# Two changes to the loads of a selective-scan kernel: the order of four partition quarters, and the layout of B and C in DRAM

## The chip, the cores and the metric

The kernel runs on one core of one Trainium2 chip. The metric is the device time of one execution in microseconds (us); the median of three runs of the kernel before is 12483.95 us (12473.74 to 12504.42). A core has TensorE (PE, matrix products), VectorE (DVE), ScalarE (ACT), GpSimd (POOL) and SyncE (SP), which here only issues DMA transfers. ACT issues transfers too. Sixteen DMA engines move the data between DRAM and the on-chip memory of 128 partitions (SBUF).

## The reference, cut to what matters

Two image layers are followed by two token layers. An image layer is a selective scan over 4 images of 64 x 64 pixels in four directions (K = 4), with E = 192 channels and 16 states:

```
delta = softplus(dt_projs(dts) + bias)            # (image, direction, channel, step)
h     = exp(delta * A) * h + delta * u * B        # 16 states, one step after another
y     = sum over states of h * C  (+ u * D)
```

`u` is the convolved and activated input, read in each direction's order; B and C depend on image, direction and step. The four directions are added, normalised, gated and projected. The token layers are linear attention and a feed-forward network in quantised numbers; they aren't touched by the change.

## The kernel before, in words

Images are taken in pairs. One pair in one image layer is a *phase*; there are four, one after the other (2 pairs, 2 layers). Each has three parts: `prepare` (normalisation, convolution, projection; all results go to DRAM), `scan_phase` (the recurrence) and `finish` (summing, norm, gate, output projection), where the finish of one phase runs between the steps of the next one's `prepare`. The token layers come last.

**How the scan is tiled.** G = 8 groups (4 directions x 2 images) times 16 states make the 128 partitions. Partition 32a + 4g + s holds group g and state 4a + s, so a *quarter* of 32 partitions has all groups and four states. A *unit* is 12 channels (EB) times 512 steps (TC); a *chunk* is 16 units, all 192 channels of 512 steps; 8 chunks make the 4096 steps, 128 units a phase.

**What a unit does.** `load` fills a tile `h` of 128 x 12 x 512 numbers (3 MB in all) with delta * u: the same values for all 16 states, so every quarter takes the same 8 rows of DRAM, each repeated for four partitions. POOL multiplies h by B (`times_b`, L406, four instructions of three channels). PE spreads delta to all partitions (`replicate`, L412), ACT takes exp(A * delta) in place (`decay`, L416), DVE runs the recurrence along 512 steps (`scan`, L423, one instruction per channel). PE contracts h with C (`contract`, L441), ACT evicts (`evict`, L453), SP stores y in four transfers (`store`, L461).

**du in DRAM.** `steps` writes delta * u twice, as copies 0 and 1, one on ACT's queue and one on SP's (L319). `load_quarters` (L396) reads quarter 0 from copy 0, quarter 3 from copy 1, and quarters 1 and 2 in one transfer from both copies, quarter 1 from copy 0 and quarter 2 from copy 1. Each is split into two halves of six channels: two transfers of 768 KB and four of 384 KB per unit. The order is in L387.

**B and C in DRAM.** `steps` writes 32 rows of 512 numbers, B's 16 states and C's 16, to `ph.bc[chunk][group]` by ACT's queue (L301), one transfer for each group. In the scan, `load_b` and `load_c` fetch a chunk's B or C as four transfers of 64 KB on SP, one per quarter (L344).

**What sets the order.** In `scan_phase` the program order is kept on each engine, so SP's order is as written: at the last channel (n = 11) of unit `at`, four stores of y of unit at−1; in some units a load of b (unit 8 of a chunk, for the next chunk) or of c (the last unit, for the chunk after the next); then the load of unit at+3, that is `dlt` (delta, one transfer of 288 KB, L376) and six transfers of h. The tile h has four buffers, so the load of unit at+3 takes the buffer that unit at−1 has just left. In `prepare` and `finish` a scheduler orders the instructions by its own estimates. POOL starts on a unit half a unit ahead of DVE in program order (B_LEAD = 6).

At the start of a phase SP issues: b of chunk 0, the load of unit 0, c of chunk 0, the loads of units 1 and 2, c of chunk 1 (L489 to L494).

Of the kernel before, what the change touches and what calls it, by code (L numbers as in the profile page):

```python
# [9 lines left out]
F32 = mybir.dt.float32  # L10
# [14 lines left out]
NS = 16  # L25
R = 6
K = 4
G = 2 * K
PAD = HW + 2
TC = 512  # L30
NC = L // TC
# [42 lines left out]
def rows(t):  # L74

    if len(t.shape) == 2:
        return t.rearrange("p (r w) -> p r w", w=HW)
    return t.rearrange("p h (r w) -> p h r w", w=HW)
# [49 lines left out]
class Scans:  # L128
# [19 lines left out]
    def prepare(self, ph):  # L148

        nc, cst, a, pre = self.nc, self.cst, self.a, ph.pre  # L150
        ph.gs = self.keep.tile([C, 2, 2], F32, name="gs", bufs=3)
        ph.delta = [
            self.dram.tile([NP16, G, E, TC], BF16, name="delta", bufs=2 * NC) for _ in range(NC)
        ]


        ph.du = [
            self.dram.tile([2, G, E + PITCH, TC], F32, name="du", bufs=2 * NC) for _ in range(NC)
        ]
        ph.bc = [self.dram.tile([G, 2 * NS, TC], F32, name="bc", bufs=2 * NC) for _ in range(NC)]  # L160
        ph.ud = self.dram.tile([C, 2, HW, 2, 64], F32, name="ud")
        ph.y = self.dram.tile([64, G, 2, 2, NEB, 16 * EB], F32, name="y")
        x = ph.x_in[ph.pair]

        with self.tc.tile_pool(name="prep", bufs=1) as wp, self.tc.tile_pool(
            name="steps", bufs=2
        ) as sp:

            def load(name, shape, at=0):
                t = wp.tile([at + shape[0]] + shape[1:], F32, name=name)  # L170
                nc.sync.dma_start(t[at:], a[pre + name])
                return t

            xp = load("x_proj", [C, 2, 2, XD2])
            dt_w = load("dt_w", [XD2 - 2 * NS, 2, E], at=2 * NS)
            conv_b = load("conv_b", [C, 2])
            ds = load("Ds", [C, 2, K])
            dsum = wp.tile([C, 2], F32, name="dsum")
            nc.vector.tensor_reduce(dsum, ds, mybir.AxisListType.X, ALU.add)
            yield  # L180


            st = wp.tile([C, 2, 8, 6], F32, name="st")
            with self.tc.tile_pool(name="stats", bufs=2) as rp:
                for hl in range(8):
                    raw = rp.tile([C, 8, 2, 64], F32, name="raw")
                    nc.sync.dma_start(raw, x[:, hl * 8 : hl * 8 + 8])
                    for i in range(2):
                        nc.vector.bn_stats(st[:, i, hl], raw[:, :, i])
                    yield  # L190
            for i in range(2):
                mv = wp.tile([C, 2], F32, name="mv")
                nc.vector.bn_aggr(mv, st[:, i].rearrange("p c s -> p (c s)"))
                ps = self.bank()
                nc.tensor.matmul(ps[:C, :1], cst.group, mv[:, 0:1], start=True, stop=True)
                gs = ph.gs[:, i]
                nc.vector.tensor_copy(gs[:, 0:1], ps[:C, :1])
                d = wp.tile([C, 1], F32, name="d")
                nc.vector.tensor_tensor(d, mv[:, 0:1], gs[:, 0:1], ALU.subtract)
                nc.vector.scalar_tensor_tensor(d, d, d, mv[:, 1:2], ALU.mult, ALU.add)  # L200
                ps = self.bank()
                nc.tensor.matmul(ps[:C, :1], cst.group, d, start=True, stop=True)
                ln = wp.tile([C, 2], F32, name="ln")
                neg_rsqrt(nc, cst, ps[:C, :1], ln[:, 0:1], gs[:, 1:2], ln[:, 1:2])
                nc.vector.tensor_scalar_mul(gs[:, 1:2], gs[:, 1:2], -1.0)
                yield
            in_w = wp.tile([C, E], F32, name="in_w")
            nc.sync.dma_start(in_w, a[pre + "in_proj_w"][:, :E])
            taps = wp.tile([C, 9, E], F32, name="taps")
            nc.sync.dma_start(taps, a[pre + "conv_w"].unsqueeze(0).broadcast_to([C, 9, E]))  # L210

            nc.vector.tensor_tensor(
                taps, taps, in_w.unsqueeze(1).broadcast_to([C, 9, E]), ALU.mult
            )

            xc = [wp.tile([C, 2, L], F32, name="xc", bufs=2) for _ in range(2)]
            yield from self.convolve(ph, 0, x, xc[0], taps, conv_b, dsum)
            ph.beside = 0.5
            other = self.convolve(ph, 1, x, xc[1], taps, conv_b, dsum)
            for i in range(2):  # L220
                for c in range(NC):
                    for k in range(2):
                        yield from self.steps(ph, sp, xc[i], xp, dt_w, i, k, c)
                        for _ in range(2):
                            next(other, None)
                            yield
                for _ in other:
                    yield
                ph.beside = 1.7
# [52 lines left out]
    def steps(self, ph, sp, xc, xp, dt_w, i, k, c):  # L282


        nc, cst = self.nc, self.cst
        u = scan_view(xc, k, c)
        ps = self.bank()
        for h in range(2):
            nc.tensor.matmul(rows(ps[:XD2]), xp[:, k, h], u[:, h], start=h == 0, stop=h == 1)  # L289
        xd = sp.tile([XD2, TC], F32, name="xd")  # L290

        nc.scalar.activation(xd[:XD], ps[:XD], AF.Identity, bias=cst.one_row[:XD])  # L292
        nc.scalar.activation(
            xd[64:], view(ps[64:XD2], TC - 1, (-1, TC)), AF.Identity, bias=cst.one_row[64:]
        )
        yield
        both = []
        for back in range(2):
            at = 64 * back
            g, cc = 2 * (k + 2 * back) + i, NC - 1 - c if back else c  # L300
            nc.scalar.dma_start(ph.bc[cc][g], xd[at : at + 2 * NS])  # L301
            both.append((g, cc, scan_view(xc, k + 2 * back, cc), self.p_d.tile([C, 2, TC], F32, name="d")))
        for m in range(2):
            for back, (_, _, _, ps) in enumerate(both):
                part = slice(64 * back + 2 * NS, 64 * back + XD)
                nc.tensor.matmul(  # L306
                    ps[:, m], dt_w[part, k, m * C : (m + 1) * C], xd[part], start=True, stop=True
                )
        yield
        for g, cc, u, ps in both:  # L310
            delta = sp.tile([C, 2, TC], F32, name="dl")
            parts = sp.tile([C, NP16, 2, TC], BF16, name="parts")
            du = sp.tile([C, 2, TC], F32, name="du_sb")
            nc.scalar.activation(delta, ps, AF.Softplus)  # L314
            nc.scalar.copy(parts[:, 0], delta)
            nc.vector.tensor_tensor(rows(du), rows(delta), u, ALU.mult)  # L316
            nc.vector.tensor_tensor(delta, delta, parts[:, 0], ALU.subtract)  # L317
            for copy, queue in enumerate((nc.scalar, nc.sync)):
                queue.dma_start(ph.du[cc][copy, g, :E].rearrange("(h e) t -> e h t", h=2), du)  # L319
            nc.gpsimd.tensor_copy(parts[:, 1], delta)  # L320
            nc.vector.tensor_tensor(parts[:, 2], delta, parts[:, 1], ALU.subtract)  # L321
            for h in range(2):
                nc.scalar.dma_start(
                    ph.delta[cc][:, g, h * C : (h + 1) * C].rearrange("n q t -> q n t"),
                    parts[:, :, h],
                )
            yield
# [10 lines left out]
        ph.carry = self.keep.tile([128, E], F32, name="carry")  # L338
        ph.b, ph.c, ph.cw = {}, {}, {}

    def load_states(self, t, of):

        for a in range(4):
            self.nc.sync.dma_start(t[32 * a : 32 * a + 32], of[:, 4 * a : 4 * a + 4])  # L344

    def load_b(self, ph, c):
        ph.b[c] = self.units.tile([128, TC], F32, name="b")
        self.load_states(ph.b[c], ph.bc[c][:, :NS])

    def load_c(self, ph, c):  # L350
        ph.c[c] = self.units.tile([128, TC], F32, name="c")
        self.load_states(ph.c[c], ph.bc[c][:, NS:])

    def weights(self, ph, c, op):

# [25 lines left out]
    def load(self, u):  # L381

        nc, ph = self.nc, u.ph
        u.h = self.units.tile([128, EB, TC], F32, name="h", bufs=4)
        self.load_delta(u)
        n = EB // 2
        for first, quarters in ((1, 2), (0, 1), (3, 1)):  # L387
            for e in range(0, EB, n):
                self.load_quarters(u, e, n, first, quarters)

# [593 lines left out]
```

## Time and profile before

| What | us |
|---|---|
| median of 3 runs | 12483.95 |
| profiled execution, its own time | 12443.48 |
| its span, first to last instruction | 12441.7 |
| PE busy | 10107.0 |
| DVE busy | 9376.9 |
| POOL busy | 7386.0 |
| ACT busy | 7185.6 |
| the four scan phases together | 7660 |
| the parts before, between and after them | 4755 (the last, 1206, holds the token layers) |

The page gives one profiled execution. A group of instructions is named by its line, its engine and the tiles it writes and reads (`h<-du` is a transfer from du to h); behind the bar stand its busy time, the mean ns of one, and the idle time of its engine just before it with what ended most of it. The chain is found by going back from the last instruction to whatever released it, again and again; "SPq" is time in which SP issues or waits.

### The profile page before, as it was taken

The page shows a single profiled execution, that of the slowest core. Times are in us where ns is not written, and L with a number is a line of the kernel's source. Part 1 is how long each engine was busy: PE and PEld are TensorE (multiplying, and loading weights), DVE is VectorE, ACT ScalarE, POOL GpSimd, SP SyncE. Part 2 cuts the span into 40 slices and gives each one's busy share as a digit, 9 for nine tenths or more (in the row PEclk, how much of TensorE's full clock was granted, in tenths as well). Part 3 has the DMA queues.
Part 4 walks back from the last instruction along what each step waited for, and adds up shares of the span by engine and source line. Part 5 has one row for each costly group of instructions (what it writes and reads, how often), then busy time and mean ns, then how long its engine had stood idle before and what let it go on. Part 6 is the DMA issues. An engine that isn't in the chain of part 4 may idle for free.

```text
span 12441.7 us, 340858 instructions
## 1 busy us (share of the span) xinstructions
PE 10107.0 (81%) x147008; PEld 4972.1 (40%) x147008; DVE 9376.9 (75%) x9235; ACT 7185.6 (58%) x11815; POOL 7386.0 (59%) x2316
## 2 busy tenths in 40 slices
PE   7758888879878888879878888888878888887777
PEld 2224444433334444433334444443334444444333
DVE  2479999963569999982469999992459999993567
ACT  2456666644456666653456666663446666662556
POOL 0159999950149998960139899880129989990000
PEclk8665565669675555659775656558776655557787
DMA  3567676754667676764566777664567666663110
GB/s 92 172 227 247 244 248 247 248 168 140 213 205 246 245 247 244 250 200 128 176 215 244 246 247 249 243 226 125 174 202 249 244 243 245 245 244 122 30 21 11
DMA packets 882704, 2491.45 MB, mean 200 GB/s; under 512 B 279058, under 2 KB 561840, under 8 KB 737456
## 3 DMA queue, kind: packets, MB, share of 16 engines
q1 hardware_dynamic: 552496, 2163.38, 50.6%
q10 hardware_dynamic: 328704, 306.26, 8.5%
q8 instruction: 1158, 18.97, 0.7%
q14 instruction: 346, 2.83, 0.1%
HBM read 1955.42 MB, written 513.80 MB: 198 GB/s over the span
## 4 chain that ended last, share of the span: by engine, by line
DMA 53%; PE 20%; SPq 8%; DVE 7%; ACT 4%; issue 4%; POOL 3%; ACTq 1%; POOLq 0%; DVEq 0%
DMA h<-du 47%; PE c L260 8%; SPq L396 7%; POOL h L406 3%; PE f L591 2%; DVE h L423 2%; PE d L306 2%; DMA yk<-y 1%; PE c L289 1%; PE f L600 1%; POOL parts L320 1%; PE f L682 1%; DMA du<-du_sb 1%; PE y L441 1%; DVE parts L321 1%
## 5 line engine op out<-in xcount | busy, mean ns | idle before, releaser
L406 POOL TENSOR_TENSOR h<-h,b 128x1536 f32<-128x1536 f32 x2048 | 7016.6, 3456 | 780.6 <-DMA h<-du 369.0
L423 DVE TENSOR_TENSOR_SCAN h<-a,carry,h 128x512 f32<-128x512 f32 x5376 | 6356.7, 1259 | 391.8 <-POOL h L406 360.9
L416 ACT ACTIVATE a<-a,a_col 128x512 f32<-128x512 f32 x6144 | 4030.3, 662 | 1966.6 <-PE a L412 1814.4
L441 PEld LDWEIGHTS y<-h,cw 128*32 128x32 f32 x131072 | 2886.3, 145 | 3597.6 <-issue 1606.1
L441 PE MATMUL y<-h,cw 128*32 128x48 f32 x131072 | 3702.1, 269 | 438.0 <-ACT a L416 216.9
L412 PE MATMUL a<-dlt,rep 24*128 24x512 bf16 x6144 | 3319.4, 551 | 884.8 <-DVE h L423 782.1
L320 POOL CAST parts<-dl 96x1024 bf16<-96x1024 f32 x256 | 341.3, 1348 | 3092.1 <-DVE dl L317 2785.6
L316 DVE TENSOR_TENSOR du_sb<-dl,xc 96x1024 f32<-96x1024 f32 x256 | 397.3, 1577 | 1296.2 <-ACT dl L314 1234.8
L453 ACT COPY d<-y 128x384 f32<-128x384 f32 x2048 | 979.6, 478 | 485.7 <-PE y L441 432.7
L260 PE MATMUL c<-xn,taps 96*96 96x512 f32 x2304 | 1034.1, 609 | 73.5 <-DVE xn L245 71.0
L423 DVE TENSOR_TENSOR_SCAN h<-a,h 128x512 f32<-128x512 f32 x768 | 869.6, 1201 | 189.0 <-ACT a L416 110.6
L412 PEld LDWEIGHTS <-rep 24*128 24x128 bf16 x6144 | 471.9, 101 | 903.6 <-issue 451.0
L306 PE MATMUL d<-xd,dt_w 7*96 7x512 f32 x1024 | 520.8, 859 | 254.9 <-ACT xd L292 225.6
L260 PEld LDWEIGHTS c<-xn,taps 96*96 96x96 f32 x2304 | 382.6, 167 | 707.5 <-issue 628.7
L823 POOL MEMSET tn<- 1x4096 f32 x8 | 27.8, 3506 | 865.0 <-PE pa L843 514.7
L267 ACT ACTIVATE xc<-c,conv_b 96x512 f32<-96x512 f32 x128 | 87.3, 682 | 718.1 <-PE c L260 633.2
L591 PE MATMUL f<-yk,perm 128*128 128x384 f32 x1024 | 415.9, 546 | 99.6 <-DMA yk<-y 88.8
L314 ACT ACTIVATE dl<-d 96x1024 f32<-96x1024 f32 x256 | 252.0, 1017 | 400.9 <-DMA delta<-parts 234.5
L321 DVE TENSOR_TENSOR parts<-dl,parts 96x1024 bf16<-96x1024 f32 x256 | 366.9, 1455 | 153.2 <-POOL parts L320 153.1
L289 PE MATMUL c<-xc,x_proj 96*103 96x512 f32 x512 | 420.2, 958 | 4.2 <-ACT xc L267 4.2
L306 PEld LDWEIGHTS d<-xd,dt_w 7*96 7x96 f32 x1024 | 151.7, 212 | 542.4 <-ACT xd L292 295.8
L360 ACT ACTIVATE cw<-c,gmask 128x256 f32<-128x256 f32 x512 | 287.9, 573 | 126.2 <-DMA h<-du 65.9
(114 smaller groups left out, 5650.6 us busy)
## 6 DMA issues: line engine op xcount, KB each, us to landing
h<-du SPq DMA_DIRECT2D x1024, 768.0 KB
h<-du SPq DMA_DIRECT2D x2048, 384.0 KB
delta<-parts ACTq DMA_DIRECT2D x512, 288.0 KB
dlt<-delta SPq DMA_DIRECT2D x512, 288.0 KB
du<-du_sb SPq DMA_DIRECT2D x256, 384.0 KB
du<-du_sb ACTq DMA_DIRECT2D x256, 384.0 KB
y<-d SPq DMA_DIRECT2D x2048, 48.0 KB
yk<-y SPq DMA_DIRECT2D x256, 384.0 KB
```

The lines of the kernel that those rows point to most:

```text
L260: nc.tensor.matmul(rows(ps[:C]), taps[:, tap, h * C : (h + 1) * C], xn[:, ROWS * c + dy : ROWS * (c + 1) + dy, dx : dx + HW], start=tap == ...
L289: nc.tensor.matmul(rows(ps[:XD2]), xp[:, k, h], u[:, h], start=h == 0, stop=h == 1)
L306: nc.tensor.matmul(ps[:, m], dt_w[part, k, m * C : (m + 1) * C], xd[part], start=True, stop=True)
L321: nc.vector.tensor_tensor(parts[:, 2], delta, parts[:, 1], ALU.subtract)
L396: self.nc.sync.dma_start(u.h[32 * first : 32 * (first + quarters), e : e + n].rearrange("p e t -> p (e t)"), source.rearrange("a g e t -> ...
L406: self.nc.gpsimd.tensor_tensor(h, h, b, ALU.mult)
L412: self.nc.tensor.matmul(u.a[n], rep, u.dl[:, n], start=True, stop=True)
L416: self.nc.scalar.activation(u.a[n], u.a[n], AF.Exp, scale=u.ph.a_col[:, at : at + 1])
L423: self.nc.vector.tensor_tensor_scan(u.h[:, n], u.a.pop(n), u.h[:, n], 0.0 if u.c == 0 else u.ph.carry[:, at : at + 1], ALU.mult, ALU.add,)
L441: self.nc.tensor.matmul(view(u.y[32 * j : 32 * j + 32], l2 * EB, (8 * EB, 4), (1, EB)), u.ph.cw[u.c][:, l1, 8 * j + l2], view(u.h, 64 * l1 ...
L453: self.nc.scalar.copy(u.d[:, :, :, l1], u.y[:, : 32 * EB].rearrange("p (t h x) -> p t h x", t=4, h=2))
L591: nc.tensor.matmul(ps[:, : 4 * C].rearrange("p (w v e) -> p w v e", w=4, v=nv), cst.perm[:, k], view(t, off, (sw if k < 2 else -sw, 4), (1 ...
```

## The change

In `load` the quarters are taken in the order 1 and 2, 3, 0, where it was 1 and 2, 0, 3. In DRAM, B and C of a chunk lie as (quarter of the states, group, state in the quarter, step), B's four quarters before C's four, which is the order of the 128 partitions; a load of B or C is then one contiguous transfer of 256 KB, where it was four of 64 KB. The store that writes one group's rows writes eight pieces of four rows each, where it was one piece of 32 rows.

```diff
-        ph.bc = [self.dram.tile([G, 2 * NS, TC], F32, name="bc", bufs=2 * NC) for _ in range(NC)]
+        ph.bc = [self.dram.tile([NS // 2, G, 4, TC], F32, name="bc", bufs=2 * NC) for _ in range(NC)]
...
-            nc.scalar.dma_start(ph.bc[cc][g], xd[at : at + 2 * NS])
+            nc.scalar.dma_start(ph.bc[cc][:, g], xd[at : at + 2 * NS])
...
-    def load_states(self, t, of):
-
-        for a in range(4):
-            self.nc.sync.dma_start(t[32 * a : 32 * a + 32], of[:, 4 * a : 4 * a + 4])
+    def load_states(self, ph, c, first, name):
+
+        t = self.units.tile([128, TC], F32, name=name)
+        of = ph.bc[c][first : first + NS // 4]
+        self.nc.sync.dma_start(t, of.rearrange("a g s t -> (a g s) t"))
+        return t
 
     def load_b(self, ph, c):
-        ph.b[c] = self.units.tile([128, TC], F32, name="b")
-        self.load_states(ph.b[c], ph.bc[c][:, :NS])
+        ph.b[c] = self.load_states(ph, c, 0, "b")
 
     def load_c(self, ph, c):
-        ph.c[c] = self.units.tile([128, TC], F32, name="c")
-        self.load_states(ph.c[c], ph.bc[c][:, NS:])
+        ph.c[c] = self.load_states(ph, c, NS // 4, "c")
...
-        for first, quarters in ((1, 2), (0, 1), (3, 1)):
+        for first, quarters in ((1, 2), (3, 1), (0, 1)):
             for e in range(0, EB, n):
                 self.load_quarters(u, e, n, first, quarters)
```

## The prediction

> **What bounds the kernel now.** I first read the page's groups and its chain, then cut the span at the four scan phases, then followed one load cycle inside a phase. Windows have a fixed column order: length, busy time of PE, PE's weight loads, DVE, ACT and POOL, granted clock, share of the 16 DMA engines, GB/s.
>
> ```profile
> DMA 53%; PE 20%; SPq 8%; DVE 7%; ACT 4%; issue 4%; POOL 3%; ACTq 1%; POOLq 0%; DVEq 0%
> ...
> L406 POOL TENSOR_TENSOR h<-h,b 128x1536 f32<-128x1536 f32 x2048 | 7016.6, 3456 | 780.6 <-DMA h<-du 369.0
> L423 DVE TENSOR_TENSOR_SCAN h<-a,carry,h 128x512 f32<-128x512 f32 x5376 | 6356.7, 1259 | 391.8 <-POOL h L406 360.9
> ```
>
> DMA carries the chain, POOL waits for `h<-du`, and DVE waits for POOL. So the recurrence on DVE is starved by the loads of delta·u. The windows of the four scan phases say by how much:
>
> ```profile
> 775.00:2684.00 1909.00, 1621.64 (x34042) 832.57 (x34041) 1805.52 (x1536) 1305.54 (x2268) 1740.52 (x508) 0.60 0.70 245
> 3613.00:5524.00 1911.00, 1624.24 (x34042) 833.32 (x34041) 1806.32 (x1536) 1306.72 (x2269) 1740.56 (x509) 0.60 0.70 244
> 6462.00:8374.00 1912.00, 1625.12 (x34042) 832.86 (x34041) 1806.35 (x1536) 1307.18 (x2268) 1740.75 (x508) 0.60 0.70 244
> 9307.00:11235.00 1928.00, 1626.64 (x34042) 833.21 (x34041) 1806.62 (x1536) 1307.57 (x2267) 1740.52 (x508) 0.60 0.69 242
> ```
>
> DVE needs 1806 us of each 1909 to 1928, 7225 of 7660 in all: 435 us is what the loads cost, and the most that they can give back. POOL needs 1740, so it is not the bound behind DVE. In units (128 a phase) the mean period is 14.93 us; a unit that finds its data takes 14.1.
>
> Now one cycle of the chain, in time order (start, length, what):
>
> ```profile
> 4387.85 12.59 DMA h<-du
> 4400.44 0.02 issue
> 4400.45 0.69 SPq L396
> 4401.14 0.04 issue
> 4401.18 0.67 SPq L396
> 4401.85 0.04 issue
> 4401.90 0.64 SPq L396
> 4402.54 0.04 issue
> 4402.59 11.83 DMA h<-du
> ```
>
> The sixth load of one unit lands at 4400.44, and only then is the third of the next issued; three issues later comes the sixth again. A transfer waits for the one issued eight before it: eight semaphores (100 to 107) go round over SP's transfers. I call the six loads of a unit h0, h1 (middle quarters), h2, h3 (quarter 0) and h4, h5 (quarter 3). From the trace's semaphore updates I took the last update of each and the step from one landing to the next, averaged over all units: `dlt` 1.51, h0 1.68, h1 1.93, h2 1.88, h3 1.90, h4 1.89, **h5 2.79**, four stores of y 1.09. The sum is 14.66 us per unit. The odd one is h5, 0.91 above its neighbours of equal size.
>
> Why it is odd, again as windows:
>
> ```profile
> 4395.10:4396.70 1.60, 1.40 (x22) 0.28 (x16) 1.60 (x2) 1.25 (x4) 1.58 (x1) 0.50 0.51 215
> 4397.50:4400.20 2.70, 2.44 (x35) 0.83 (x34) 2.70 (x3) 1.82 (x4) 2.38 (x1) 0.50 0.97 278
> ...
> 3609.70:3611.20 1.50, 0.00 (x0) 0.00 (x0) 0.00 (x0) 1.49 (x4) 1.50 (x1) 0.50 1.06 385
> 3611.60:3613.40 1.80, 0.00 (x0) 0.00 (x0) 0.14 (x1) 1.79 (x3) 1.42 (x1) 0.50 0.82 184
> ```
>
> In the first, quarter 3 loads alone: 8 of 16 engines, 215 GB/s, 12,288-byte packets of 462 ns. In the second, h5 has company, the next unit's h0: 16 engines busy but only 278 GB/s, packets of 700 to 800 ns. The other two are from the start of phase 1, where a later unit's middle load also runs early: beside quarter **0** of the unit before it, 385 GB/s at 462 ns a packet; then beside quarter **3**, 184 GB/s at 800 to 960 ns. So the quarter decides, not the number of busy engines.
>
> [...] a quarter (8 groups to 32 partitions), `dlt`, b and c have 8 engines' updates, the middle ones 16. [...] the upper eight run ahead into the next h0. [...]
>
> **The change, part by part.**
>
> *Order 12, 3, 0.* Same transfers, bytes and issues; h2, h3 become quarter 3 and h4, h5 quarter 0. POOL's first multiplication still waits for h4. h0 of the next unit is issued when h3 lands (eight before it), so its upper half runs beside h4, h5[...]. I take 1.88 for h5: 14.66 − 0.91 = 13.75 us a unit. Bounds: 2.79 (no effect) and 1.84 (the median of h3 and h4). Below 14.1, DVE is the bound and what is left is slack.
>
> *One load of b or c for four.* Each set of four adds, per landing steps, 0.21 + 3×0.50 and makes the following `dlt` step 3.49 instead of 1.51, together 3.7 us; for c 0.22 + 1.50 + (3.07 − 1.51) = 3.3. The large term is the eight semaphores: four small transfers use up four places, so the next h0 is issued 4×1.85 us later [...]. A phase has 7 of b and 6 of c after the start: 45 us. Check: 128×14.66 + 45 = 1922, against phases of 1909 to 1928. With one transfer (128 rows of 2 KB at the measured 0.10 us, 8 rows per engine) I take 0.5 us each: 6.5 us a phase. Bounds 0 and 3.7 (no gain). SP also issues 6 fewer at 0.66 us per chunk; SP is waiting then anyway. At each phase start three issues fewer stand ahead of the first unit: 3×0.7 = 2 us, four times, on the path.
>
> *Stores of bc.* Eight groups of 4 rows instead of 32 rows: 8 engines instead of 16, so 4 rows of 0.10 us instead of 2, +0.2 us on a landing of 2.5. 256 of them would be 51 us if all were on the path. The answer on the tile bc puts all waits that end with its transfers at 163 us, 77 of them in the scans, so I take 0: what covers the stores is the convolutions on PE, 8% of the chain; without them, up to the 51. ACT's and DVE's order in the preparation shifts by a handful of instructions, and the instruction count of each is unchanged: 0 within 5 us.
>
> **Sum**, against the profiled execution, 12443.5 us (span 12441.7). DMA per phase: 128×13.75 + 6.5 = 1767, under DVE's 1806. DVE's idle is 581 us at scans; 146 of it lies before the phases' first scans and stays, so the 435 of the windows can go. I keep back 5 us per phase in the first chunk, whose scans are shorter (1.20 us, 13.4 a unit, below POOL's 13.7 and the loads' 13.75), and 1 us for each of the 28 later chunks: 48. With the 8 us at the starts the gain is 435 − 48 + 8 = 395: 12048. The median of the runs is 12484, 40 above the profiled one; the same 40 gives **12089**.
>
> **Rivals.**
>
> - *Only company counts (DRAM, any 16 engines).* h5 stays 2.79. Then DMA per phase is 128×14.66 + 6.5 = 1883 instead of 1922: 39 a phase, 156 and the 8: 12484 − 164 = 12320. [...] Against: 385 GB/s beside quarter 0.
> - *The loads become bound by buffer release.* h has four buffers; loads of unit n+3 wait for the contraction of n−1. When DMA is no longer late, SP issues four stores (0.66 each), `dlt` and h0 after each release, and engines idle meanwhile. h4 must land 24.7 us after the release (two units of 14.1 less POOL's 3.5); it would land after some 15 (issues 3.9, first packets 1.5 after an issue, as at 4395.90, and five loads of 1.9). If that slack fails, half of the gain goes: 12290.
> - *Slower: the meeting moves to h2, h3.* If the upper engines finish h1 later than the lower ones, quarter 3, now directly behind, meets them instead, and in both halves. Price: at the phase start a half of quarter 3 took 3.5 us under full overlap, +1.6; twice, 13.75 + 3.2 = 17 us a unit, 128×17 = 2176 per phase, some +260: 13530. It decides from an added 1.2 us a unit (14.93 − 13.75) on. Against: by the trace the upper engines' updates of h1 come before the lower ones' today (4403.3 to 4403.9 beside 4404.2 to 4406.1), and they have less to do.
> - *Nothing:* both edits hidden, 12484; the landing steps speak against it.
>
> **How the numbers follow.** Forecast 0.84; company 0.05; release 0.05; slower 0.03; nothing 0.03. Differences under 0.3% (37 us) can't be told from none. Faster 0.84 + 0.05 + 0.05 = 0.94, same 0.03, slower 0.03. The range leaves out all but the forecast (0.16): below, all 435 and 8 give 12041; above, the forecast with a third of the gain missing, 12220, plus 20 for the scatter of the runs.
>
> **What would show it.** Right: DVE's idle time at the scans falls from 581 to under 220, POOL's wait for `h<-du` with it; h5's step near 1.9 and no packets of 750 ns beside it; `dlt` after b near 1.5; phases of 1810 to 1825; chain no longer 47% `h<-du`. Wrong: h2 or h3 takes 2.8 or more; h5 stays; or POOL still starts each unit 0.16 us after h4 lands.

## The result: slower by 2.4%

The changed kernel takes 12794.26 us (median of 4 runs, 12753.37 to 12831.11), the kernel before 12488.62 us (median of 4 runs, the three named above among them). The ratio is 1.0244, 95% interval 1.0209 to 1.0279. The forecast was 12089.

From the page of the changed kernel, the lines that answer to those shown of before:

```profile
DMA 59%; PE 18%; SPq 9%; DVE 5%; ACT 4%; issue 3%; POOL 1%; ACTq 1%; DVEq 0%; POOLq 0%
...
L406 POOL TENSOR_TENSOR h<-h,b 128x1536 f32<-128x1536 f32 x2048 | 7007.4, 3452 | 1149.5 <-DMA h<-du 382.7
L423 DVE TENSOR_TENSOR_SCAN h<-a,carry,h 128x512 f32<-128x512 f32 x5376 | 6358.3, 1259 | 706.9 <-POOL h L406 691.8
```

DVE and POOL do the same work in the same time (7231 us of DVE in the scan phases, 7225 before). What grew is their waiting: DVE's idle time before these scans from 391.8 to 706.9, POOL's from 780.6 to 1149.5. The loads are still the bound, and they are slower. The windows of the four scan phases (columns as in the prediction) show where:

```profile
771.40:2776.00 2004.60, 1653.84 (x34042) 839.67 (x34041) 1807.15 (x1537) 1314.61 (x2268) 1739.78 (x509) 0.56 0.69 233
3712.90:5725.50 2012.60, 1665.44 (x34042) 841.51 (x34041) 1807.63 (x1537) 1316.71 (x2268) 1739.68 (x509) 0.55 0.69 232
6656.90:8662.80 2005.90, 1659.61 (x34042) 841.08 (x34041) 1808.79 (x1536) 1315.21 (x2267) 1739.08 (x509) 0.56 0.69 233
9595.30:11600.30 2005.00, 1659.36 (x34042) 840.77 (x34041) 1807.88 (x1536) 1315.70 (x2267) 1739.67 (x509) 0.56 0.69 233
```

The phases are 2005 to 2013 us long, were 1909 to 1928, together 8028 in place of 7660: 368 us more, of a span that grew by 363. All of the loss is in the scans; preparation, finish and token layers are as they were.

The chain inside a phase has the same form, with longer pieces (start, length, what):

```profile
4402.52 14.54 DMA h<-du
4417.06 0.02 issue
4417.08 0.69 SPq L396
4417.77 0.04 issue
4417.81 0.67 SPq L396
4418.48 0.04 issue
4418.52 0.65 SPq L396
4419.17 0.04 issue
4419.21 13.52 DMA h<-du
```

The landing steps, worked out from the trace's semaphore updates as in the prediction (means in us). I take an update for the end of one engine's part. A quarter, `dlt` and a load of 64 KB have eight updates at the landing, besides one about 1.1 us after the issue; h0, h1 and the stores of y have 16. The stores show two sets of engines: of their 16 updates eight come 1.8 to 1.9 us after the issue (medians of before), and the other eight of the first store follow the eight of h5, each taken in its order, by 0.2 us (median). "Lower" engines are the eight that every transfer of the scan uses, "upper" ones the other eight; "lag" is how far the slowest lower engine lands behind the median of the eight at h2, and "dlt behind y" is the step of `dlt` where only the stores of y stand before it:

| kernel | h0 | h1 | h2 | h3 | h4 | h5 | dlt behind y | dlt behind b | lag |
|---|---|---|---|---|---|---|---|---|---|
| before (0 before 3, four loads) | 1.68 | 1.93 | 1.88 | 1.90 | 1.89 | 2.79 | 1.51 | 3.49 | 1.7 |
| changed (3 before 0, one load) | 1.65 | 1.92 | 1.92 | 1.93 | 2.62 | 2.81 | 1.86 | 2.20 | 2.9 |

Three things stand out. The edit to b and c does what it should: `dlt` behind b fell from 3.49 to 2.20. The swap doesn't: h5 is as slow as it was, and h4 has become slow too. And one engine of the eight now lands 2.9 us behind their median, about one and a half transfers; the second slowest is 0.9 behind. With the stores the steps of a unit sum to 15.72 us, and a unit's share of the measured phases is 15.68.

### The profile page after: what moved, and what is told of

Same layout as the page of the kernel before. It is cut to its first block, busy times and chain, and to the rows that moved or that the text cites. A ratio compares the mean times of both kernels' runs of the same rounds, so it can differ in the third digit from the quotient of the medians.

```text
span 12804.5 us, 340674 instructions
## 1 busy us (share of the span) xinstructions
PE 10263.5 (80%) x147008; PEld 5008.4 (39%) x147008; DVE 9380.5 (73%) x9235; ACT 7220.8 (56%) x11815; POOL 7376.3 (58%) x2316
## 4 chain that ended last, share of the span: by engine, by line
DMA 59%; PE 18%; SPq 9%; DVE 5%; ACT 4%; issue 3%; POOL 1%; ACTq 1%; DVEq 0%; POOLq 0%
DMA h<-du 54%; SPq L396 8%; PE c L260 8%; PE f L591 2%; PE d L306 2%; DMA yk<-y 1%; DMA delta<-parts 1%; PE c L289 1%; POOL parts L320 1%; PE f L600 1%; PE f L682 1%; DMA du<-du_sb 1%; PE f L671 1%; DVE parts L321 1%; DVE dl L317 1%
## 5 line engine op out<-in xcount | busy, mean ns | idle before, releaser
L406 POOL TENSOR_TENSOR h<-h,b 128x1536 f32<-128x1536 f32 x2048 | 7007.4, 3452 | 1149.5 <-DMA h<-du 382.7
L423 DVE TENSOR_TENSOR_SCAN h<-a,carry,h 128x512 f32<-128x512 f32 x5376 | 6358.3, 1259 | 706.9 <-POOL h L406 691.8
L412 PE MATMUL a<-dlt,rep 24*128 24x512 bf16 x6144 | 3445.6, 568 | 1121.5 <-DVE h L423 1030.2
```

The costliest lines, as they stand in the source:

```text
L406: self.nc.gpsimd.tensor_tensor(h, h, b, ALU.mult)
L412: self.nc.tensor.matmul(u.a[n], rep, u.dl[:, n], start=True, stop=True)
L423: self.nc.vector.tensor_tensor_scan(u.h[:, n], u.a.pop(n), u.h[:, n], 0.0 if u.c == 0 else u.ph.carry[:, at : at + 1], ALU.mult, ALU.add,)
```

## The experiments

Each ratio is to runs of the kernel before that were measured beside it, with its 95% interval in brackets; e1 to e4 ran on one chip, e5 to e10 on another.

**1. Which of the two edits did it.** The two are taken apart: in the first kernel the old order is kept with the new layout of B and C, in the second only the order is swapped.

```diff
 # e1: after, with
-        for first, quarters in ((1, 2), (3, 1), (0, 1)):
+        for first, quarters in ((1, 2), (0, 1), (3, 1)):
 # e2: before, with
-        for first, quarters in ((1, 2), (0, 1), (3, 1)):
+        for first, quarters in ((1, 2), (3, 1), (0, 1)):
```

> The new layout and single loads of B and C, with the old order of the quarters (0 before 3). In the changed kernel the step of dlt behind a load of b fell from 3.49 to 2.20 us and behind c from 3.07 to 2.13, while the steps of h4 and h5 rose to 2.62 and 2.81. Theory 'the order did it': this is faster than before, 12484 less about 150 (6 of 7 us per chunk saved, 26 chunks), 12330 to 12400; h5's step stays 2.8, h4's 1.9. Rival 'the single transfer of b or c did it' (256 KB on all 16 engines, and the eight semaphores shifted): near the changed kernel, 12700 or more, with h4's step above 2.4.

> Only the order of the quarters is changed (3 before 0), B and C as before. Theory 'the order did it': slower than the changed kernel, since the gain of b and c is missing: 12850 to 12950; steps of h4 2.6, of h5 2.8, dlt behind b above 3.4. Rival 'b and c did it': within 0.5% of before.

Measured: e1 12435.48 us, 0.9944 of before (0.9923 to 0.9964); e2 12719.24, 1.0177 (1.0158 to 1.0195). So the order did most of it. Without the swap (e1) h4 and h5 take 1.97 and 2.89 us; with the swap alone (e2), 2.43 and 2.59. The new layout alone is a small gain, a third of the 150 us expected. But the effects don't add: 0.9944 times 1.0177 is 1.012, and the two together measure 1.0244. The swap alone missed its expectation in the same way (12850 to 12950 were expected since a gain would be missing; it was faster than both edits together). Experiment 4 takes this up.

**2. Source or destination.** Quarter 0 and quarter 3 differ in what they read (copy 0 or 1 of du) and in where they write. Crossing the copies parts the two.

```diff
-        copies = slice(0, 2) if quarters == 2 else slice(first % 2, first % 2 + 1)
+        copies = slice(0, 2) if quarters == 2 else slice(1 - first % 2, 2 - first % 2)
```

e3 is this in the kernel before, e4 in the swapped one (e2).

> The kernel before, but quarter 0 reads copy 1 of du and quarter 3 reads copy 0; destinations, order, sizes as before. The last quarter of a unit (3) now reads copy 0, as the last quarter (0) of the changed kernel does. Theory 'DRAM side' (it counts which copy the last quarter reads): as slow as the swapped order, 12750 or more, h4's step above 2.4. Theory 'SBUF side' (it counts which partitions the last quarter writes): as before within 0.5%, h5 2.8, h4 1.9.

> Only the order swapped (3 before 0) with the copies crossed too: the last quarter (0) reads copy 1. Theory 'DRAM side': like the kernel before, 12484 within 0.5%. Theory 'SBUF side': like the swapped order alone, 12750 or more.

Measured: e3 12489.37 us, 0.9997 (0.9988 to 1.0005); e4 12709.02, 1.0169 (1.0149 to 1.0190), as e2 (a little under the 12750 expected, like e2 itself). h4 and h5 take 1.89 and 2.89 us in e3, as in the kernel before. Which copy is read counts for nothing here; of the two differences, the partitions that the last quarter writes are left.

**3. Whom quarter 0 meets.** The lag gives the hint. When the slow engine works on h4 and h5, the other seven are a transfer or two ahead, at the next `dlt` (in the changed kernel an h4 has its last update at 4415.24, and seven of the next `dlt` come from 4414.20 to 4414.95). Over 1984 landing steps of h2 to h5 I fitted the slow engine's step to the time in which the others did something else beside it (a fit over one trace for each kernel, with the start of a transfer taken 1.95 us behind its issue; it explains 82% and 84% of the variance). It is a lead and no proof: a step that is long for any reason also meets more company.

| added us per us of company | kernel before (last quarter 3) | changed (last quarter 0) |
|---|---|---|
| other lower engines at `dlt` (partitions 0 to 23) | −0.01 | 0.50 |
| other lower engines at h0 | 0.00 | −0.11 |
| upper engines at h0 | 0.40 | 0.17 |

By the fit, `dlt` slows quarter 0 (0.50) and not quarter 3 (−0.01), and the upper engines at h0 slow quarter 3 (0.40) more than quarter 0 (0.17). `dlt` writes partitions 0 to 23, quarter 0 writes 0 to 31, quarter 3 96 to 127. My guess was that the partitions decide which company costs; the fit doesn't show it, and of h0, which writes 32 to 95, the trace doesn't show which engine writes which. The first test moves `dlt` to partitions 64 to 87, away from quarter 0, in the changed kernel (e5) and in the kernel before (e6); the second leaves it where it is and changes when it is loaded, behind the first half of quarter 3, so that the engines ahead and behind then write quarter 3, which `dlt` at 0 to 23 didn't slow in the fit (e7).

```diff
 # e5 (after) and e6 (before)
-        u.dl = self.units.tile([NP16 * G, EB, TC], BF16, name="dlt", bufs=3)
+        u.dl = self.units.tile([64 + NP16 * G, EB, TC], BF16, name="dlt", bufs=3)[64:]
...
-        rep = self.cst.rep[: NP16 * G]
+        rep = self.cst.rep[64 : 64 + NP16 * G]
 # e7 (after)
-        self.load_delta(u)
         n = EB // 2
...
                 self.load_quarters(u, e, n, first, quarters)
+                if first == 3 and e == 0:
+                    self.load_delta(u)
```

> The changed kernel with the tile of delta at partitions 64 to 87 in place of 0 to 23. In the changed kernel the last engine's steps of h4 and h5 (quarter 0) grow by 0.50 us for each us in which the other seven engines load delta, and by 0.17 for each in which the upper engines load h0; in the kernel before (quarter 3 last) 0.0 and 0.40. [...] h4 and h5 fall from 2.62 and 2.81 to 2.0 or less. Delta then meets the upper engines' h0 instead, some 0.6 us on 1.4, so a unit of 15.7 becomes about 14.8: 12400 to 12600. Rival 'any company of dlt' (its DRAM reads, or too many engines at once): no change, 12750 to 12850, h4 and h5 stay above 2.5.

> The kernel before (quarter 3 last) with delta at partitions 64 to 87. [...] delta now meets quarter 3 and the upper engines' half of h0[...]: slower than before by at least 1.5%, 12680 to 13000, with steps of h4 above 2.2 and of dlt above 2.0. Rival 'any company of dlt': as before within 0.5%.

> The changed kernel with the load of delta moved behind the first half of quarter 3, [...] h4 and h5 fall to 2.0 or less without a new meeting: a unit of 15.7 less 1.7, about 14.1, where VectorE's 14.1 takes over: 12100 to 12250, below the kernel before. Rival 'any company of dlt': the growth moves to h2 or h3, 12650 or more.

Measured: e5 12550.17 us, 1.0057 (1.0037 to 1.0077); e6 13256.68, 1.0634 (1.0609 to 1.0658); e7 11999.59, 0.9621 (0.9607 to 0.9635), against 12471.83 of before measured beside them. The same move of `dlt` helps the swapped order by 1.8% and costs the old order 6.3%, more than expected. In steps: e5 brings h4 from 2.62 to 1.92 and h5 from 2.81 to 2.61 only, above the 2.0 expected. e6 has h4 at 2.27 and h5 at 3.96, where quarter 3 now has both `dlt` and the upper engines as company; the step of `dlt` behind y is 1.30, not above 2.0 as expected.

The four traces show the meeting at h4 without the weakness of the fit. Company is counted here only in the first 1.85 us of the step, the length of an undisturbed one, and there no upper engine is at h0 yet. "Mostly" means that the other seven engines spend over 0.6 us of it at `dlt` on average. The slow engine's step of h4, means in us (number of steps):

| last quarter, place of `dlt` | others hardly at `dlt` (under 0.1 us) | others mostly at `dlt` |
|---|---|---|
| before: quarter 3, `dlt` at 0 to 23 | 1.89 (376) | 1.88 (20) |
| changed: quarter 0, `dlt` at 0 to 23 | 1.97 (200) | 3.34 (150) |
| e5: quarter 0, `dlt` at 64 to 87 | 1.90 (341) | 1.94 (53) |
| e6: quarter 3, `dlt` at 64 to 87 | 2.05 (383) | 3.23 (49) |

With `dlt` at 0 to 23 the meeting costs quarter 0 (0 to 31) 1.37 us, and at 64 to 87 it costs quarter 3 (96 to 127) 1.18; crossed, the steps differ by 0.04 us at most. No other place of `dlt` was tried.

In e7, which ends below the range expected, the steps of h4 and h5 are 1.90 and 1.92, the lag is 1.6, and the stall is gone. From its page, then its four scan phases:

```profile
L407 POOL TENSOR_TENSOR h<-h,b 128x1536 f32<-128x1536 f32 x2048 | 7019.8, 3462 | 279.2 <-DMA h<-du 126.2
L424 DVE TENSOR_TENSOR_SCAN h<-a,carry,h 128x512 f32<-128x512 f32 x5376 | 6318.1, 1270 | 4.9 <-POOL h L407 4.6
```

```profile
776.50:2573.30 1796.80, 1525.08 (x34042) 821.95 (x34041) 1796.75 (x1537) 1282.28 (x2268) 1743.02 (x509) 0.73 0.70 260
3512.40:5316.20 1803.80, 1535.08 (x34042) 823.11 (x34041) 1796.92 (x1537) 1285.56 (x2268) 1743.18 (x509) 0.71 0.70 259
6253.80:8052.00 1798.20, 1524.92 (x34042) 821.92 (x34041) 1795.23 (x1536) 1281.50 (x2267) 1743.91 (x509) 0.73 0.70 260
8991.90:10789.90 1798.00, 1527.05 (x34042) 822.39 (x34041) 1795.51 (x1536) 1282.20 (x2267) 1743.14 (x509) 0.73 0.70 260
```

DVE's 706.9 us of waiting before these scans are 4.9: each phase is as long as DVE's own work, but for 7 us in the second. The granted clock is higher here (0.71 to 0.73 in the phases, 0.55 to 0.56 in the changed kernel), but that isn't the reason: seven runs of the kernel before beside e8 to e10 had clocks from 0.654 to 0.783 at 12470 to 12508 us, and e10 below is slow at 0.795. The same bytes move at 260 GB/s, 233 in the changed kernel. DVE's timeline of a stretch inside a phase shows it at a glance, first the changed kernel, then e7:

```profile
4384.92 14.21 DVE L423 TENSOR_TENSOR_SCAN h<-a,carry,h 128x512 f32<-128x512 f32 x12 [1.95 <-POOL h L406]
4401.44 14.21 DVE L423 TENSOR_TENSOR_SCAN h<-a,carry,h 128x512 f32<-128x512 f32 x12 [2.31 <-POOL h L406]
4419.04 14.21 DVE L423 TENSOR_TENSOR_SCAN h<-a,carry,h 128x512 f32<-128x512 f32 x12 [3.39 <-POOL h L406]
```

```profile
4279.74 101.13 DVE L424 TENSOR_TENSOR_SCAN h<-a,carry,h 128x512 f32<-128x512 f32 x86
```

Whether the place of `dlt` in the queue gives this by itself is asked in e10: the kernel before with `dlt` between the two halves of quarter 3, which comes last there. And e9 is e7 without the new layout of B and C.

> The kernel before, quarter 3 last, with delta between the two halves of quarter 3 and no other change. [...] quarter 3 still meets the upper engines' half of the next h0, so little is gained: 12350 to 12650. Rival 'the place of delta in the queue alone gives the gain': below 12200.

> The swapped order with delta inside quarter 3, but B and C as before the change. [...] the four loads cost 7 us of the loads' time per chunk, [...]: 12000 to 12100. Rival 'the single loads carry the gain': 12200 or more.

Measured: e10 12793.33 us, 1.0238 (1.0213 to 1.0263); e9 12052.93, 0.9651 (0.9631 to 0.9671). The place alone is no gain: with the old order it loses 2.4%. It loses more than I expected (12350 to 12650). The steps point to `dlt`, which now meets quarter 0 there: the slow engine, 2.8 us behind, is still at h3 (quarter 0's second half) when the others reach `dlt`, and h3's step is 2.42 where it was 1.90; h5, now later, meets more of the upper engines' work and takes 3.31. With the swap, e9, the gain is there without the new layout. With it, e7, the ratio is 0.3% lower, but the two intervals overlap. So neither the swap (e2, 1.0177) nor the place of `dlt` (e10, 1.0238) gains by itself; the two together do (e9, 0.9651).

**4. Why the layout of B and C helps one order and hurts the other.** With four loads the engines run dry for a moment behind each set (the 3.49 us of `dlt` behind b). By unit of a chunk, the lag at h2 falls to 1.1 us there in the swapped kernel (e2) and climbs to 3.3 before the next set; with one load it never falls below 2.2. So the pause that the edit takes away would be what lets the slow engine catch up. e8 puts three useless loads of 2 KB behind each single load in the changed kernel.

```diff
         self.nc.sync.dma_start(t, of.rearrange("a g s t -> (a g s) t"))
+        pad = self.units.tile([32, 3, 16], F32, name="pad")
+        for i in range(3):
+            self.nc.sync.dma_start(pad[:, i], of[i, :, :, :16].rearrange("g s t -> (g s) t"))
```

> The changed kernel with three loads of 2 KB behind each single load of B or C, so that four transfers again stand between two units there, as before the change. They move nothing that is used. With the four loads the slowest engine's lag behind the median of the eight fell to 1.1 us behind each load of b or c (swap alone), with one load it stays at 2.2 and more. Theory 'the pause lets the slow engine catch up': faster than the changed kernel in spite of more transfers, near the swap alone, 12680 to 12760, dlt behind b again above 3.0. Rival 'the 256 KB load on 16 engines costs by itself': 12790 to 12850.

Measured: e8 12692.93 us, 1.0160 (1.0134 to 1.0186), below the changed kernel's 1.0244 with intervals apart: three more transfers with nothing to do make it 101 us faster (medians; the kernels before, measured beside each, differ by 10). The lag falls to 1.2 behind the loads again, and `dlt` behind them takes 3.23. DVE's periods by unit, from the one behind the loads of c on (without the first chunk), are 17.0, 15.0, 15.1, 14.9, 15.9, 15.9, 16.1 us; in the changed kernel 16.1, 15.9, 15.9, 15.5, 15.7, 16.2, 15.5. There the pause costs 0.9 us once and saves 0.6 to 0.9 in each of the next three.

## Why the prediction was wrong

- *What bounds the kernel: right.* The loads of du starved DVE, by 435 us at most, and only the scan phases moved. e7 takes 472 us off (11999.59 against 12471.83), more than 435, since DVE's own work shrank by 10 us a phase as well.
- *"Beside quarter 0, 385 GB/s": right as far as it went.* The company of the upper engines costs quarter 0 little: in e7 h5, quarter 0, takes 1.93 us beside them and 1.89 without; in the kernel before h5, quarter 3, takes 2.91 and 1.92 (over 1.2 and under 0.1 us of company in the first 1.85 us, with the earlier eight of the 16 updates of h0 and h1 taken as the upper engines'). I read from these windows that quarter 0 is free, but they held only that one company.
- *The step that failed: "Order 12, 3, 0 ... so its upper half runs beside h4, h5".* I listed what runs beside quarter 3 in the last place and didn't list what would run beside quarter 0 there. `dlt` goes to partitions 0 to 23 by the same eight engines (the prediction itself counts it among the transfers with 8 engines' updates), and only four small stores stand between h5 and it in the queue. Quarter 0 in the last place meets it; h4 and h5 took 2.62 and 2.81 where I had 1.89 and 1.88, and `dlt` behind y took 1.86 where I had 1.51. That makes the sum of a unit 15.72 us instead of 13.75. The upper bound given for h5 (2.79) is where h5 ended, but it left h4 out, and so reached no loss.
- *Why I didn't see the meeting.* I averaged the last update of each transfer and took the eight engines as one. They aren't in step: the last one lagged by 1.7 us in the kernel before, so transfers that follow each other in the queue also run beside each other. The window that I read as quarter 3 alone (4395.10 to 4396.70) still holds the slowest engine's quarter 0, whose last update is at 4395.82. The chain sees the last engine alone.
- *The rival on the slower side: right sign, wrong place, too large.* It had the meeting move to h2, h3 and the upper engines, and 13530 us; h2 and h3 stayed at 1.92 and 1.93. That the kernel came out slower doesn't make this rival right.
- *B and C: mechanism right, size off.* `dlt` behind b fell to 2.20, and c likewise. By itself this gave 0.56% where the steps promised about 1.2%, because the steps of the slow engine grew: in e1 h4 from 1.89 to 1.97 and h5 from 2.79 to 2.89, by an estimate from these steps 92 us over the 512 units. `dlt` behind b was also to be near 1.5; it took 2.46 in e1. With the swap the edit turned into a loss of 0.7% (the changed kernel against e2), and e8, which puts the pause back, takes this loss away.
- *The stores of bc at nothing: held.* Their updates are eight at the landing in place of 16, they land 2.65 us after the issue in place of 2.52 (medians), and an issue on ACT's queue takes 646 ns in place of 320; the preparation did not grow for it.
- *"Right or wrong" list:* DVE's waiting rose instead of falling, h5's step stayed, and phases of 2005 to 2013 us excluded the forecast. The list named "h2 or h3", not h4.

What stays open: which of the eight engines lags, and why; the trace doesn't name a packet's engine, and that it is the same one throughout is inferred from its being last at every step. Why h5 in e5 still took 2.61, though `dlt` was then at 64 to 87: it took 1.88 beside `dlt` alone and 2.79 beside `dlt` and the upper engines' h0, so the place of `dlt` doesn't explain all that company costs. And why e6 lost so much more than its two meetings suggested. What it is in the chip that makes two ranges of partitions disturb each other isn't shown either; the runs show that it doesn't matter which copy of du is read (e3, 0.9997), that it matters which partitions are written (e5 and e6, 1.0057 and 1.0634), and that `dlt` at 0 to 23 disturbs quarter 0 and at 64 to 87 quarter 3.

## What to carry to other kernels

When transfers share engines and a few semaphores, list for each one every transfer that is one or two places before or behind it, and compare all their destinations, those of the same queue too; an engine that lags (here by 2.9 us, one and a half transfers) makes neighbours in the queue into neighbours in time. A pause is not always waste (e8, which puts it back, is 101 us faster than the changed kernel): find out what catches up in it before removing it. And follow the slowest engine of a transfer, since that one's landing is what everyone waits for: in the kernel before an h5 has its last update at 4400.43, and SP issues the next load at 4400.45.

## What the runs showed of the hardware that was not expected

- With the same bytes and, but for b and c, the same number of transfers, the order of the loads and the partitions of one of them (`dlt`) moved the time of the whole kernel between 0.962 (e7) and 1.063 (e6) of before.
- The slowest engine's part of a 384 KB load took over 1 us longer when other engines wrote `dlt` to partitions 0 to 23 beside quarter 0 (3.34 us for 1.97) or to 64 to 87 beside quarter 3 (3.23 for 2.05), and no longer when the two were crossed (1.94 for 1.90 and 1.88 for 1.89; h4 in the table of experiment 3).
- Three added loads of 2 KB per set made the changed kernel 0.8% faster (12692.93 us in e8 for 12794.26).
- SP's issue of a load of b takes 329 ns as one transfer over 16 engines (256 KB, 16 updates), and took 662 ns as one of 64 KB over 8 (eight updates at the landing). The number of engines isn't all: h0 and h1, over 16 too, take 590 ns to issue.
